# Second convolution by halves at its first and last channels, scan's first token piece loaded in parts, its first delta rows made by TensorE

## The chip, the cores and the metric

The kernel runs on one core of one Trainium2 chip. The core has five engines with instruction queues of their own: TensorE (PE in the profile, with PEld for its weight loads), VectorE (DVE), ScalarE (ACT), GpSimd (POOL) and SyncE (SP), which here only issues DMAs. Each queue is worked off in order: an instruction that waits for a semaphore holds all that stand behind it on its engine. The metric is the device time of one execution in microseconds (us), the median of three runs.

## What is computed

Two layers on a batch of 32 images of 96 channels, 56 by 56, all float32.

```python
# layer 0: depthwise 7x7, layer norm over channels, MLP 96 -> 384 -> 96, residual
h = conv_depthwise_7x7(x) + conv_b
h = layernorm_over_channels(h) * ln_g + ln_b
h = gelu(h @ w1 + b1) @ w2 + b2
x = layer_scale * h + x
# layer 1: depthwise 5x5, SiLU, selective scan over L = 3136 tokens
x = silu(conv_depthwise_5x5(x) + conv_b)
xs = x.reshape(B, C, L)
dts, Bs, Cs = split(einsum('kd,bdl->bkl', x_proj_w, xs))      # 6, 4, 4 rows
delta = softplus(einsum('dr,brl->bdl', dt_w, dts) + dt_b)
log_dA = maximum(delta * A, log(1e-9))                          # A: 96 x 4
P = exp(cumsum(log_dA))
hs = P * cumsum(delta * Bs * xs / maximum(P, 1e-9))
y = einsum('bdnl,bnl->bdl', hs, Cs) + xs * Ds
```

## The kernel before

The work has four stages one after the other: first convolution, MLP, second convolution, scan. Between stages the data pass through DRAM. A framework places buffers and semaphores; instructions that the code passes to `pin` keep the program's order on their engine, the others are placed by a scheduler.

**MLP (L487 to L589).** 28 groups of four image rows of half the batch. Half h = 0 is done first, then h = 1; within a half, `group(n)` (L152) gives row 0, 4, ... 24, each for two parts of the batch. Each group runs `hidden` (PE, then Gelu on ACT) and `result` (PE, then DVE adds bias and residual into a tile `o`). After the second part of a row group, POOL issues four DMAs for each of three channel blocks (L564), twelve in all, of 240 KB each, to `block_d`. Row m of `block_d` is (1 - h) * 28 + row + i: the first half fills rows 28 to 55, the second rows 0 to 27 upwards, so rows 24 to 27 come last. Rows stand in reverse: a high row of `block_d` is a low row of the image.

**Second convolution (L596 to L684).** 96 channels. `load_channel(c)` issues on SP the channel's taps (`wt`, L614, 128 KB) and two loads of 30 rows from `block_d` (`xq`, L626, 225 KB each): half h = 0 reads rows 26 to 55, half 1 rows 0 to 29. There are four pairs of `xq` buffers, zeroed once by DVE (L605), since the loads leave edges free. `convolve(c)` is 32 matmuls (L638), 16 for each half; `activate(c)` is one SiLU of 128 x 896 out of PSUM on ACT (L652); `beside` copies four residues of the columns into `st` (L661), one copy by ACT and three by DVE; `store_channel(c)` writes `conv2_d` (L667, 392 KB). `st` and `yt` have three buffers. The loop (L672) gives SP, for each c, the load of channel c + 2 and then the store of channel c - 2; both are on one queue, so the store stands behind that load and the next load behind the store.

**Scan (L692 on).** Tokens are taken in pieces of two images by 28 rows (`load(p)`, L723, tile `xs`); piece 0 goes by two DMAs on SP, one for each image. Each image of a piece makes three units of 128 rows: 32 channels by 4 states, 1568 tokens. For a unit:

- PE makes `pz` (L744) from the tokens, ACT turns it into delta by Softplus (L752), delta times token is made (L758; by DVE for the first image, by POOL after), and both are stored to `du_d` in DRAM (`keep_du`, L761)
- `spread_du` (L805) loads them back as `rep`, each channel's row four times, so that 128 rows stand side by side
- ACT's `decay` makes Exp, Relu, Identity of the delta rows (L810 to L812); POOL's `drive` multiplies the product rows by `bt` (L816); `bt` is spread by PE (L791) from rows that PE (L770) and a copy by ACT (L779) have made, and copied by ACT (L795)
- DVE runs two scans and one elementwise step (L826, L829, L833) through `pv` in PSUM, which is zeroed first (L699); POOL multiplies by `ct` (L845), PE sums (L855, L863), ACT copies and stores

The first image has its own sequence at L887 to L918. Its delta rows are stored and loaded back by themselves, ahead of the products: SP has the two delta stores, `spread_du(0, deltas)`, the two product stores, `spread_du(0, products)`, the rows of units 1 and 2 (both parts in one DMA each), then piece 1's tokens.

The loop and SP's order around the change:

```python
        for c in range(-2, C + 2):
            if c + 2 < C:
                load_channel(c + 2)
            if 0 <= c - 2:
                store_channel(c - 2)
            if 0 <= c < C:
                convolve(c)
...
                for h in range(2):
                    keep_du(0, h, deltas)
                spread_du(0, deltas)
                for h in range(2):
                    delta_x(0, h, nc.vector)
                    keep_du(0, h, products)
```

Of the kernel before, what the change touches and what calls it, by code (L numbers as in the profile page):

```python
# [21 lines left out]
N, R = 4, 6  # L22
# [27 lines left out]
def convnext_then_scan_kernel(  # L50
# [58 lines left out]
    dsm_t = const.tile([C, C], F32, name="dsm_t")  # L109

# [41 lines left out]
    def group(n):  # L152

        h, m = divmod(n, groups // 2)
        return h, m // 2 * RB, m % 2
# [20 lines left out]
    with tc.tile_pool(name="prep", bufs=1) as prep, tc.tile_pool(name="c1", bufs=4) as pool, tc.tile_pool(  # L176
# [145 lines left out]
        def scan_rows():  # L322
# [5 lines left out]
            for k in range(4):  # L328
                rows = slice(32 * k, 32 * k + 2 * N)
                at = 32 * k + (k // 2) * N  # L330
                kept(nc.vector.tensor_copy,
                    pick_t[rows].rearrange("p (d n) -> p d n", n=N),
                    ident[rows, at : at + N].rearrange("p (o n) -> p o n", o=1).to_broadcast(
                        [2 * N, DG, N]
                    ),
                )
            kept(nc.vector.tensor_reduce,
# [149 lines left out]
    with tc.tile_pool(name="mlp_g", bufs=14) as pool_g, tc.tile_pool(  # L487
# [46 lines left out]

        def result(n, s, d):
# [25 lines left out]
            if p == 1 and s == 1:  # L561
                m = (1 - h) * QR + row
                for i in range(RB):
                    nc.gpsimd.dma_start(  # L564
# [28 lines left out]

    with tc.tile_pool(name="c2", bufs=3) as pool, tc.tile_pool(  # L596
        name="c2k", bufs=1
    ) as keep, tc.tile_pool(name="c2_ps", bufs=4, space=PSUM) as psum:
# [4 lines left out]
        for t in xqs:  # L603
            for h in range(2):
                nc.vector.memset(t[h], 0.0)  # L605
# [4 lines left out]
        def load_channel(c):  # L610
            wt = pool.tile([128, RW * QC * 2], F32, name=f"wt2_{c}", tag="wt", bufs=4)
            taps = taps2_d[c, 0, 0:1, 0:1]
            step = QC * 2
            pin(nc.sync.dma_start(  # L614
                wt,
                bass.AP(
                    taps.tensor, taps.offset,
                    [[step, RW], [2 * RW * step, QC], [1, RW * step]],
                ),
            ))  # L620
            wts[c] = wt
            for h in range(2):
# [8 lines left out]
        def convolve(c):  # L631
            wv = wts.pop(c).rearrange("p (o f t) -> p f t o", f=QC, t=2)
            ps = psum.tile([128, 2, 512], F32, name=f"ps2_{c}", tag="ps")
            for h in range(2):
                xv = xqs[c % len(xqs)][h].rearrange("p (b r) -> p b r", r=QP)
                for t in range(2):
                    for f in range(QC):
                        pin(nc.tensor.matmul(  # L638
                            ps[RW * f : RW * f + RW, h, : B * QW].rearrange(
# [8 lines left out]
            pss[c] = ps  # L648

        def activate(c):  # L650
            yt = pool.tile([128, 2, B * QW], F32, name=f"yt_{c}", tag="yt")
            pin(nc.scalar.activation(  # L652
                yt, pss.pop(c)[:, :, : B * QW], AF.Silu, bias=c2b_t[:, c : c + 1], scale=1.0
            ))
            st = pool.tile([QR, 2, B, QW, QC], F32, name=f"st_{c}", tag="st")
            sts[c] = yt, st

        def beside(c, f, copy):

            yt, st = sts[c]  # L660
            pin(copy(  # L661
                st[:, :, :, :, f],
                yt[RW * f : RW * f + QR].rearrange("p h (b q) -> p h b q", q=QW),
            ))

        def store_channel(c):
            pin(nc.sync.dma_start(  # L667
                conv2_d[c].rearrange("(h o) w -> o h w", h=2),
                sts.pop(c)[1].rearrange("p h b q f -> p h (b q f)"),
            ))  # L670

        for c in range(-2, C + 2):  # L672
            if c + 2 < C:
                load_channel(c + 2)
            if 0 <= c - 2:
                store_channel(c - 2)
            if 0 <= c < C:
                convolve(c)
            if 0 <= c - 1 < C:
                beside(c - 1, 0, nc.scalar.copy)  # L680
            if 0 <= c < C:
                activate(c)
                for f in range(1, QC):
                    beside(c, f, nc.vector.tensor_copy)  # L684
# [7 lines left out]
    with tc.tile_pool(name="sc", bufs=2) as pool, tc.tile_pool(  # L692
# [10 lines left out]
        xts: dict = {}  # L703
# [9 lines left out]
        HQ = H // NCH  # L713
# [9 lines left out]
        def load(p):  # L723
            b, q = place(p * NI)
            xt = pool.tile([C, HQ, NI * W], F32, name=f"xs_{p}", tag="xs", bufs=3)
            rows = conv2_d[:, q * HQ : (q + 1) * HQ, b * W : (b + NI) * W]
            for i in range(1 if p else NI):
                cols = slice(None) if p else slice(i * W, (i + 1) * W)
                pin(nc.sync.dma_start(xt[:, :, cols], rows[:, :, cols]))
            xts[p] = xt  # L730

        def tokens(k, s, n):
# [3 lines left out]
            return xts[p][:, s * hh : (s + 1) * hh, i * W : (i + 1) * W]  # L736
# [40 lines left out]
        def rows_out(k):  # L777
            bn = pool.tile([128, 2, BK], F32, name=f"bn_{k}", tag="bn")
            pin(nc.scalar.copy(bn, bns[k][:, :, :BK]))  # L779
# [27 lines left out]
        def decay(i):  # L807

            g, da = i % NG, reps[i][:, 0, :]
            pin(nc.scalar.activation(da, da, AF.Exp, scale=a_t[:, g : g + 1]))  # L810
# [3 lines left out]
        def drive(i):  # L814
            ut = reps[i][:, 1, :]
            pin(nc.gpsimd.tensor_mul(ut, ut, bts[i // NG]))  # L816
# [66 lines left out]
        for i in range(-12, units + 1):  # L883
# [3 lines left out]
            if p == 0 and at == 0:  # L887
# [11 lines left out]
                spread_du(0, deltas)  # L899
                for h in range(2):  # L900
                    delta_x(0, h, nc.vector)
                    keep_du(0, h, products)
                rows_bc(0)
                rows_out(0)
                spread_du(0, products)
                for u in range(1, NG):
                    spread_du(u)
                load(1)
                for h in range(2):
                    spread(0, 0, h)  # L910
                decay(0)
# [7 lines left out]
            if at == 3 and p + 1 < PC and (p + 1) != 1:  # L919
                load(p + 1)  # L920
# [97 lines left out]
```

## Time and profile before

| what | value |
|---|---|
| median of three runs | 3308.79 us (3304.99 to 3313.47) |
| profiled execution | 3313.1 us, its span 3311.2 us |
| PE busy | 2783.1 us (84%) |
| DVE busy | 2593.7 us (78%) |
| ACT busy | 2240.1 us (68%) |
| POOL busy | 1685.9 us (51%) |
| first matmul of the second convolution | 1188.74 us from the span's start |
| its last matmul | ends at 1522.4 us |
| first scan of unit 0 (L826) | 1558.47 us |
| DMA in the middle of the second convolution (1300 to 1400) | busy share 0.93, 285 GB/s |

A line of a group of instructions reads: source line, engine, operation, what it writes <- what it reads with shapes, count | busy time in us, mean duration in ns | idle time of its engine just before, and what ended that idle time. A line of the order of time reads: start, length, engine, line, operation, tiles, count, and in brackets the idle time before it and what released it. SPq marks SP's issuing. The 40 digits are tenths of busy time in equal slices of the span, 82.8 us each.

### The profile page before, as it was taken

The numbers are of one execution on the slowest core, as the hardware profiler recorded it, in microseconds if no ns is written. First come the engines' busy times: TensorE is split into PE (matmuls) and PEld (weight loads), VectorE is DVE, ScalarE is ACT, GpSimd is POOL, SyncE is SP. The second block draws the span as 40 slices with busy tenths as digits, with TensorE's granted clock in tenths as the row PEclk, the third lists the DMA queues.
The fourth block names the chain that finished last, engine by engine and source line by source line (L and its number), as shares of the span: only waits on it lengthen the run. The fifth ranks groups of instructions, "written<-read, shape, count | busy, mean of one in ns | idle before, by whom it ended". The sixth has DMA issues, their size and how long they took to land. (4 is left out here: it accounts for less than half of the span.)

```text
span 3311.2 us, 53717 instructions
## 1 busy us (share of the span) xinstructions
PE 2783.1 (84%) x21898; PEld 1078.3 (33%) x21898; DVE 2593.7 (78%) x1538; ACT 2240.1 (68%) x1964; POOL 1685.9 (51%) x814
## 2 busy tenths in 40 slices
PE   8999899999999989994787777777777777777775
PEld 4666333333333333332222222222222222222221
DVE  7899533333333369996899999999999999999998
ACT  4556443333333358886888788888888887879784
POOL 1000010100101000001889899999989898989896
PEclk9999899999999999997666666666766666666767
DMA  8999765555646279998888777878787877778773
GB/s 246 292 295 292 208 177 153 168 164 148 183 138 188 76 213 288 286 283 227 285 279 266 270 257 272 283 254 279 253 282 254 286 253 274 256 272 268 271 269 110
DMA packets 299254, 788.03 MB, mean 238 GB/s; under 512 B 121648, under 2 KB 192176, under 8 KB 274464
## 3 DMA queue, kind: packets, MB, share of 16 engines
q1 hardware_dynamic: 263280, 659.77, 63.2%
q10 hardware_dynamic: 26896, 82.29, 6.7%
q0 software_dynamic: 8832, 42.55, 4.5%
q8 instruction: 172, 2.82, 0.4%
q14 instruction: 74, 0.61, 0.1%
HBM read 543.58 MB, written 240.90 MB: 237 GB/s over the span
## 5 line engine op out<-in xcount | busy, mean ns | idle before, releaser
L816 POOL TENSOR_TENSOR rep<-rep,bt 128x1568 f32<-128x1568 f32 x192 | 674.4, 3513 | 378.6 <-DMA rep<-du_d 378.6
L845 POOL TENSOR_TENSOR hs<-hs,ct 128x1568 f32<-128x1568 f32 x191 | 669.5, 3505 | 100.8 <-DVE hs L833 89.2
L826 DVE TENSOR_TENSOR_SCAN pv<-rep,pv 128x1568 f32<-128x1568 f32 x192 | 664.5, 3461 | 42.4 <-ACT rep L812 25.6
L530 ACT ACTIVATE g<-ph,b1p_t 128x896 f32<-128x896 f32 x336 | 320.2, 1004 | 483.8 <-PE ph L520 483.7
L553 DVE SCALAR_TENSOR_TENSOR o<-po,b2r_t,x 128x224 f32<-128x224 f32 x336 | 190.7, 608 | 530.1 <-PE po L539 523.2
L564 POOL DMA_DIRECT2D block_d<-o x168 | 81.1, 490 | 727.7 <-DVE o L553 622.0
L520 PE MATMUL ph<-h,w1r_t 32*128 32x448 f32 x4032 | 430.2, 555 | 4.4 <-ACT hs L403 2.3
L744 PE MATMUL pz<-xs,wd_t 96*96 96x392 f32 x512 | 280.9, 715 | 171.2 <-ACT du L752 120.1
L539 PE MATMUL po<-g,w_t 128*32 128x448 f32 x4032 | 413.1, 543 | 0.0
L791 PE MATMUL pk<-bn,pick_t 8*128 8x392 f32 x1024 | 291.9, 691 | 93.3 <-ACT y L872 81.4
L863 PE MATMUL py<-hs,sel_t 128*32 128x392 f32 x1536 | 322.7, 674 | 55.0 <-POOL hs L845 54.8
L829 DVE SCALAR_TENSOR_TENSOR pv<-pv,rep 128x1568 f32<-128x1568 f32 x192 | 345.6, 1800 | 21.3 <-POOL rep L816 1.4
L833 DVE TENSOR_TENSOR_SCAN hs<-rep,carry_h,pv 128x1568 f32<-128x1568 f32 x96 | 334.1, 3480 | 10.0
L661 DVE COPY st<-yt 28x896 f32<-28x896 f32 x288 | 317.9, 1104 | 26.9 <-ACT yt L652 13.1
L638 PE MATMUL ps<-xq,wt 128*32 128x448 f32 x3072 | 307.8, 546 | 37.1 <-DMA xq<-block_d 22.8
L833 DVE TENSOR_TENSOR_SCAN hs<-rep,pv 128x1568 f32<-128x1568 f32 x96 | 328.4, 3420 | 9.6
L375 PE MATMUL ps<-xt,mat 32*64 32x432 f32 (+2 forms) x6144 | 316.4, 556 | 22.6 <-ACT mat L357 22.2
L811 ACT ACTIVATE rep<-rep,lift_t 128x1568 f32<-128x1568 f32 x192 | 307.6, 1602 | 6.3
L812 ACT ACTIVATE rep<-rep,lift_t 128x1568 f32<-128x1568 f32 x192 | 307.6, 1602 | 6.3
L810 ACT ACTIVATE rep<-rep,a_t 128x1568 f32<-128x1568 f32 x192 | 308.3, 1606 | 4.7 <-DMA rep<-du_d 4.2
L855 PE MATMUL py<-xs,dsm_t 96*96 96x392 f32 x512 | 302.4, 732 | 10.0 <-ACT ct L795 4.5
L520 PEld LDWEIGHTS ph<-h,w1r_t 32*128 32x128 f32 x4032 | 192.7, 185 | 243.6 <-issue 155.8
(111 smaller groups left out, 2807.7 us busy)
## 6 DMA issues: line engine op xcount, KB each, us to landing
rep<-du_d SPq DMA_DIRECT2D x191, 1568.0 KB, 8.1
du_d<-du SPq DMA_DIRECT2D x126, 588.0 KB, 9.1
xq<-block_d SPq DMA_DIRECT2D x192, 225.0 KB, 5.1
xt<-in_x_dram SPq DMA_DIRECT2D x192, 224.0 KB, 4.9
block_d<-o POOLq DMA_DIRECT2D x168, 240.0 KB, 4.9
h<-conv_d SPq DMA_DIRECT2D x84, 448.0 KB, 5.1
x<-in_x_dram SPq DMA_DIRECT2D x336, 112.0 KB, 2.9
conv_d<-st SPq DMA_DIRECT2D x96, 392.0 KB
```

Source lines behind the costliest of these rows:

```text
L375: nc.tensor.matmul(pss[k // 2][2 * RW * p : 2 * RW * p + 2 * RW, k % 2, :HALF].rearrange("p (i r) -> p i r", r=W2)[:, :, lo:hi], lhsT=wv[r ...
L520: pin(nc.tensor.matmul(phs[i // 2][:, i % 2, :HALF], lhsT=w1r_t[rows, d, f * 128 : (f + 1) * 128], rhs=hts[n, d][rows, s * HALF : (s + 1) ...
L530: pin(nc.scalar.activation(gt, ph[:, :, :HALF], AF.Gelu, bias=b1p_t[:, f : f + 1], scale=1.0))
L539: pin(nc.tensor.matmul(po[CB * i : CB * i + CB, :HALF], lhsT=w2_t[:, f, CB * d : CB * d + CB], rhs=gts[n, s, f, i // 2][:, i % 2], start=( ...
L661: pin(copy(st[:, :, :, :, f], yt[RW * f : RW * f + QR].rearrange("p h (b q) -> p h b q", q=QW),))
L810: pin(nc.scalar.activation(da, da, AF.Exp, scale=a_t[:, g : g + 1]))
L816: pin(nc.gpsimd.tensor_mul(ut, ut, bts[i // NG]))
L826: pin(nc.vector.tensor_tensor_scan(grown, da, zero, pv[:, last : last + 1] if q else 1.0 / EPS, ALU.mult, ALU.add))
L829: pin(nc.vector.scalar_tensor_tensor(run, in0=grown, scalar=1.0, in1=ut, op0=ALU.min, op1=ALU.mult))
L833: pin(nc.vector.tensor_tensor_scan(ht, da, run, carry_h[:, col : col + 1] if q else 0.0, ALU.mult, ALU.add))
L845: pin(nc.gpsimd.tensor_mul(ht, ht, cts[k]))
L863: pin(nc.tensor.matmul(py[g * DG : (g + 1) * DG, s, :BK], lhsT=sel_t, rhs=hss[k * NG + g][:, cols], start=False, stop=True, tile_position= ...
```

## The change

Five edits, and helpers that go with them.

1. The MLP's second half takes its rows downwards, 24 to 0, so that rows 0 to 3 of `block_d` are written last; all but the last twelve stores on POOL are pinned.
2. The second convolution works by pieces: channels 0 to 3 by half 0, then channels 0 to 3 by half 1, then channels 4 to 94 whole, then channel 95 by half 0 and half 1: 101 pieces. SP is given load n + 3 and then store n - 2. Taps are loaded with a channel's first piece.
3. The `xq` buffers are zeroed by POOL, pinned, all halves 0 first; before it was DVE.
4. Piece 0's tokens: image 0 of channels 0 to 93 is loaded after channel 94's store has been issued, ahead of channel 95's stores; channels 94 and 95 after the last store; image 1 after the first image's product stores. The token pool is opened before the second convolution.
5. Unit 0's delta rows no longer pass through DRAM: four matmuls with a matrix of ones, `each_t`, repeat each of 32 channels four times in `pv`, and ACT's Exp reads them there in two instructions. The rows of units 1 and 2 are loaded in two DMAs each, deltas first. The copy of `bn` for image 0 goes from ACT to DVE.

```diff
-        return h, m // 2 * RB, m % 2
+        return h, ((QR - RB) - m // 2 * RB if h else m // 2 * RB), m % 2
...
+            kept(nc.vector.tensor_copy,
+                each_t.rearrange("p (d n) -> p d n", n=N),
+                ident[:DG, :DG].rearrange("p (d o) -> p d o", o=1).to_broadcast([DG, DG, N]),
+            )
...
+                store = early if n < groups - 1 else nc.gpsimd.dma_start
...
+    def load_tokens(p, channels=slice(0, C), images=slice(0, NI)):
+        b, q = p // NCH * NI, p % NCH
+        if p not in pieces_x:
+            pieces_x[p] = pool_xs.tile([C, HQ, NI * W], F32, name=f"xs_{p}", tag="xs")
+        cols = slice(images.start * W, images.stop * W)
+        rows = conv2_d[channels, q * HQ : (q + 1) * HQ, b * W : (b + NI) * W]
+        pin(nc.sync.dma_start(pieces_x[p][channels, :, cols], rows[:, :, cols]))
...
-        for t in xqs:
-            for h in range(2):
-                nc.vector.memset(t[h], 0.0)
+        for h in range(2):
+            for t in xqs:
+                pin(nc.gpsimd.memset(t[h], 0.0))
...
+        pieces = [(c, (h,)) for h in range(2) for c in range(len(xqs))]
+        pieces += [(c, (0, 1)) for c in range(len(xqs), C - 1)]
+        pieces += [(C - 1, (h,)) for h in range(2)]
...
-        for c in range(-2, C + 2):
-            if c + 2 < C:
-                load_channel(c + 2)
-            if 0 <= c - 2:
-                store_channel(c - 2)
+        for n in range(-3, last + 2):
+            if n + 3 < last:
+                load_piece(n + 3)
+            if 0 <= n - 2:
+                store_piece(n - 2)
+
+            if n - 2 == last - 3:
+                load_tokens(0, slice(0, C - 2), slice(0, 1))
...
+        load_tokens(0, slice(C - 2, C), slice(0, 1))
...
+        def delta_rows():
+
+            reps[0] = pool.tile([128, 2, CH], F32, name="rep_0", tag="rep", bufs=5)
+            at = pv.rearrange("p (s q) -> p s q", q=512)
+            for h in range(2):
+                for s in range(2):
+                    pin(nc.tensor.matmul(
+                        at[:, 2 * h + s, :BK], lhsT=each_t,
+                        rhs=dus[0, h][:DG, 0, s * BK : (s + 1) * BK],
+                        start=True, stop=True, tile_position=(0, 0),
+                    ))
+                pin(nc.scalar.activation(
+                    two(reps[0][:, 0, h * HT : (h + 1) * HT]), at[:, 2 * h : 2 * h + 2, :BK],
+                    AF.Exp, scale=a_t[:, 0:1],
+                ))
...
-                spread_du(0, deltas)
                 for h in range(2):
                     delta_x(0, h, nc.vector)
                     keep_du(0, h, products)
+                load_tokens(0, images=slice(1, 2))
+                delta_rows()
                 rows_bc(0)
-                rows_out(0)
+                rows_out(0, nc.vector.tensor_copy)
                 spread_du(0, products)
                 for u in range(1, NG):
-                    spread_du(u)
-                load(1)
+                    spread_du(u, deltas)
+                for u in range(1, NG):
+                    spread_du(u, products)
+                load_tokens(1)
+                decay(0, first=False)
                 for h in range(2):
                     spread(0, 0, h)
-                decay(0)
                 drive(0)
```

## The prediction

> **What bounds the kernel now.** I read the 40 slices first, then the idle times of the second convolution's groups, then the order of time at the stage's two ends.
>
> ```profile
> PE   8999899999999989994787777777777777777775
> ...
> DVE  7899533333333369996899999999999999999998
> ...
> DMA  8999765555646279998888777878787877778773
> ```
>
> Four stages: first convolution, MLP (DVE at 3), second convolution (slices 15 to 18: PE, DVE and DMA all at 9), scan (DVE at 9 to the end). Digits 13 to 14 and 18 to 19 are the seams. The scan is DVE's: 192 units of 3461 + 1800 + 3450 ns, with hardly a gap after 1634 us, so whatever moves the first units moves the end by as much.
>
> ```profile
> L661 DVE COPY st<-yt 28x896 f32<-28x896 f32 x288 | 317.9, 1104 | 26.9 <-ACT yt L652 13.1 <-DMA conv_d<-st 8.2 <-issue 0.2
> L638 PE MATMUL ps<-xq,wt 128*32 128x448 f32 x3068 | 307.1, 546 | 25.9 <-DMA xq<-block_d 22.8 <-ACT st L661 2.0
> L661 ACT COPY st<-yt 28x896 f32<-28x896 f32 x96 | 196.7, 2049 | 59.3 <-DMA conv_d<-st 58.1
> ```
>
> In the second convolution (window 1190 to 1530) DVE is busy 317.9 of 334 us; its only removable steady idle is the 8.2 us behind landing stores. PE's waits for loads and ACT's for stores lie beside that.
>
> ```profile
> 1174.58 1.93 POOL L564 DMA_DIRECT2D block_d<-o  x4 [44.11 <-DVE o L553]
> ...
> 1178.78 4.01 DVE L605 MEMSET xq<- 128x480 f32 x8
> 1179.03 1.45 POOL L564 DMA_DIRECT2D block_d<-o  x3 [0.26 <-DVE o L553]
> 1180.63 0.49 POOL L564 DMA_DIRECT2D block_d<-o  x1 [0.15 <-issue]
> 1180.66 2.14 SPq L626 DMA_DIRECT2D xq<-block_d  x2
> ...
> 1188.74 19.88 PE L638 MATMUL ps<-xq,wt 128*32 128x448 f32 x192 [11.19 <-DMA wt<-taps_d]
> ```
>
> The first seam: the last MLP rows are issued by POOL from 1174.58 to 1181.12, SP's first load of rows waits for them until 1180.66, and PE stands 11.19 us, until that load lands (7.7 us from issue, against 5.1 in the middle: twelve stores share the engines).
>
> ```profile
> 1521.86 2.90 DVE L661 COPY st<-yt 28x896 f32<-28x896 f32 x3 [0.42 <-DMA conv_d<-st]
> ...
> 1525.18 1.76 DVE L699 MEMSET pv<- 128x2048 f32 x1 [0.42 <-issue]
> 1526.96 2.85 DVE L661 COPY st<-yt 28x896 f32<-28x896 f32 x3
> 1533.41 2.39 SPq L729 DMA_DIRECT2D xs<-conv_d  x2
> ...
> 1539.67 4.71 PE L744 MATMUL pz<-xs,wd_t 96*96 96x392 f32 x8 [17.25 <-DMA xs<-conv_d]
> ...
> 1542.61 0.91 ACT L752 ACTIVATE du<-pz,dtb_t 96x784 f32<-96x784 f32 x1 [7.69 <-PE pz L744]
> ...
> 1553.57 1.60 ACT L810 ACTIVATE rep<-rep,a_t 128x1568 f32<-128x1568 f32 x1 [3.00 <-DMA rep<-du_d]
> ...
> 1558.47 3.43 DVE L826 TENSOR_TENSOR_SCAN pv<-rep,pv 128x1568 f32<-128x1568 f32 x1 [12.14 <-ACT rep L812]
> ...
> 1559.76 3.48 POOL L816 TENSOR_TENSOR rep<-rep,bt 128x1568 f32<-128x1568 f32 x1 [378.64 <-DMA rep<-du_d]
> ```
>
> The second seam is a serial chain: last copies, store, load of tokens (lands 5.6 later), PE at 1539.67, softplus, delta to DRAM and back as 128 rows, Exp at 1553.57, first scan 1558.47. Call PE's start P. After three units DVE idles again, 9.21 us before 1595.74: there ACT had first to serve the next token piece, issued at 1556.96 behind three row loads and landed at 1573.81 (P+34.1). A gain ahead of that is kept only if this piece comes earlier too.
>
> **Part A, the front: no early start, about -1.** The change lets half 0 of channels 0 to 3 read rows that were stored long before; but the loads wait for the zeroing, now on POOL, and in the built program the last twelve stores stand ahead of the eight memsets on POOL. So the first memset begins at 1181.1, not at 1168 when the hidden layer's inputs are free. POOL's memsets took 0.36 us for 288 columns and 1.69 for 1920, so 480 are some 0.5: first load near 1181.7, 1.0 late. Given back: the first SiLU needs 16 matmuls instead of 32 (4.74 us, at a granted clock of 0.5 to 0.8), some 1.9 sooner, and takes half of 1.0. Fifteen more DVE copies (thirty halves for fifteen whole ones) cost between nothing and 0.2 us each (the smallest instruction of ACT here, one column); I take 0.5 for them and POOL's delay together, since most lie beside other waits. Then halves 1 of channels 2 and 3 are issued only between stores that wait for DVE, while the queue has slack (DMA share 0.63 between 1195 and 1200). DVE, the fullest engine, so starts its first copy (1195.91) about 1.0 - 1.9 - 0.5 + 0.5 = -0.9 us from there, -1 rounded; from -2.5 (no lateness) to +2 (the slack is lost for good).
>
> The Trainium skill (Perfetto Trace Analysis, Optimizing Scalar/DVE Operations) speaks against halves: about 60 ns of access per DVE operation on SBUF. By it the copies would cost 15 x 0.06 = 0.9 us more (estimate); no row here has a half copy.
>
> **Part B, the middle: about -2.** Loads go out one piece further ahead (n+3 for c+2), now each behind the matmuls that free its buffer; the store stays behind them on SP's queue. This could end PE's 22.8 us of waiting, but DVE comes next, and has 8.2 us to give. DMA is at 0.93 to 0.94 there (1300 to 1500), and a row load takes SP 0.93 us to issue in the median where 0.32 is the fastest: near full. The cost side: SP waiting for PE delays the store queued behind it, and the three buffers of st are freed later. I bound it by doubling the same wait, +8.2; the other end is -8.2. I take -2: the nearest row, DVE at 95% of the window, says that little can change.
>
> **Part C, the last channel and the tokens: -4.5.** Old chain from the end of channel 94's copies: 1524.76, zeroing of pv, three copies, store 1529.87, landed about 1533.3, load, 1539.01, PE 1539.67. New: half 0 of channel 95 is copied first (3 x 0.55, half of 1.1) to 1526.4, and image 0 needs only that half; then pv and half 1, to 1529.9 as before. The 94-channel load goes out at about 1525.3, when channel 93's store (1521.50) has landed in some 3.5 us as the last one did; it takes 5.6, to 1531; half 0's store is behind it on the same queue, landed near 1531.8; then two channels, 2.6 us like the fastest small transfers (wt 2.5, du 2.6), 1534.5; PE at 1535.2. If the queue didn't matter, half 1's issue (1530.2) would set it: 1532.8, PE 1533.5, -6.2. If each of the two small transfers is held as the second image's load was (landed 2.88 after the one ahead, issued 0.37 after it), some 3.5 more: only -1 is left.
>
> The skill (DMA: Bandwidth & Descriptors, Queues, rings and completion order) says that an engine consumes one ring's descriptors in order: it backs the price of standing behind the big load, and by it -4.5 rather than -6.2 (estimate).
>
> **Part D, delta rows by TensorE: -4.9.** From P, by the rows above: the two softplus start at P+2.9 and P+4.75 (1542.61, 1544.42) and take 0.91; the table for Exp takes 1.28, to P+7.0; the four matmuls of 0.7 (nearest row: bt's, 0.71) lie beside that. Two Exp out of PSUM, 0.91 each as the softplus of the same 784 columns, to P+8.8; Relu and Identity, 1.6 each, to P+12.0: first scan there, before at P+18.8. But DVE's second step needs POOL's product, and its rows still come through DRAM. Before, the products' stores stood behind the delta row load on SP, so the product rows were issued at P+15.4 (1555.11). Now DVE has made both products at P+6.65, they are stored at P+6.7 and landed 2.9 later (a lone du store took 2.57): rows issued at P+9.6. Image 1's load stands ahead of them with 2.9 us of queue, so they land at P+15.1; POOL multiplies 3.5; second step at P+18.7 instead of P+23.6. The loads behind keep their old distances (landings 1559.7, 1563.93, 1568.52, 1573.81; split in two, but the same bytes): token piece 1 at P+29.2 instead of P+34.1, and unit 3, which waits for it, moves by the same 4.9.
> Beside it lie bt's copies (to P+13.7), bn's copy on an idle DVE, and image 1's softplus (to P+18.5, then table and decay to P+24.6; unit 1's scan would start at P+24.0, and unit 3's wait swallows the 0.6). Bounds: -2 (image 1's load pushes piece 1 back by all its 2.9) to -5.8 (not at all: P+15.4 to P+9.6).
>
> **Sum.** -1 - 2 - 4.5 - 4.9 = -12.4. The profiled execution took 3313.1 (span 3311.2 and 1.9 around it): 3300.7. The median of three runs is 4.3 lower, so I forecast 3296.
>
> **Rivals.**
> 1. The middle speeds up: PE's 22.8 us of load waits go and DVE's 8.2 with them: 6.2 more than forecast, 3290. For it: PE's idle names the loads; against: DVE and DMA near full. Chance 0.2.
> 2. The tail gives little: the big token load holds the last half's store and the two channels (C -1), and piece 1 doesn't come much earlier (D -2): -1 - 2 - 1 - 2 = -6, 3303. Several transfers in one queue speak for it, the lone landings of 2.5 us against. 0.23.
> 3. Slower: SP, now waiting for matmuls ahead of each load, issues the stores later, the three buffers of st come free later, and ACT (58.1 us of such waits already) and DVE lose that in each whole channel. A, C and D give 10.4, so it decides from 10.4 / 91 = 0.11 us for each of the 91; at 0.2 it is +18 - 10 = +8, 3317. Against: PE runs some 8 us ahead of the stores (channel 8: matmuls end 1218.8, store 1226.7), so its matmuls should be done when SP asks. 0.09.
> 4. The change does start the front early (memsets ahead of the stores): up to 8 more, 3288. The order on POOL speaks against. 0.03.
>
> **Numbers.** Forecast 0.45. A measurement can tell 0.3%, 9.9 us, from no change: faster means under 3298.9. The forecast lies just below, so two thirds of its 0.45 count as faster (0.30), with rivals 1 and 4 (0.23) and a little of rival 2: 0.56. Slower by as much is the larger part of rival 3, 0.05; the rest, 0.39, is no change. Range: all best ends are -2.5 - 8.2 - 6.2 - 5.8 = -22.7, 3286; at the other side 3309, no gain, beyond rival 2; most of rival 3 is left out.
>
> **What would show it.** A: memsets on POOL after 1181, PE's first matmul of the stage within 1 us of 1188.7. B: DVE idle in the middle near 8. C: PE's pz some 4.5 us nearer to the last matmul of the stage. D: first scan at P+12, second step P+18.7, the 9 us wait before unit 3 still there. Wrong if memsets run at 1168, if copies wait for stores more than before, or if piece 1 lands later than P+31.

## The result and the profile after

The changed kernel took 3326.7 us (median of four runs, 3323.6 to 3329.4), the kernel before 3311.1 beside it: 1.0046 times as long, 95% interval 1.0032 to 1.0061. The forecast was 3296, its range ended at 3309. With every execution of the kernel before that was run for this study (139, in six groups with medians from 3310.5 to 3312.4) its median is 3311.3, so the change costs 15.4 us. Executions of one kernel spread over 6 to 20 us; differences between two experiments therefore carry an interval, 95% by resampling the executions.

The profiled execution has a span of 3324.8 us, 13.6 more than before. In the 40 slices the stages look as before; at the second seam DVE's digit falls from 6 to 5 and DMA's from 8 to 6. Its timeline at the first seam, in the columns start, time, engine, line, tiles, count, [idle before and what ended it]:

```profile
1178.87 1.45 POOL L575 DMA_DIRECT2D block_d<-o  x3 [0.27 <-DVE o L562]
...
1181.02 3.59 POOL L632 MEMSET xq<- 128x480 f32 x8
1181.56 0.37 SPq L659 DMA_DIRECT2D xq<-block_d  x1
...
1188.88 10.42 PE L672 MATMUL ps<-xq,wt 128*32 128x448 f32 x84 [11.49 <-DMA xq<-block_d]
...
1194.15 4.91 DVE L698 COPY st<-yt 28x448 f32<-28x448 f32 x8 [15.58 <-ACT yt L687]
```

Up to here it is part A as forecast: zeroing behind the stores on POOL, PE 0.1 us later than before, DVE's first copy 1.8 us sooner. But the 1.8 us are lost again within the eight halves. DVE's timeline before (first line) and after:

```profile
1195.91 44.52 DVE L661 COPY st<-yt 28x896 f32<-28x896 f32 x39 [13.12 <-ACT yt L652]
...
1210.68 1.92 DVE L698 COPY st<-yt 28x448 f32<-28x448 f32 x3 [3.35 <-DMA conv_d<-st]
```

Before, 39 copies follow one another without a wait. After, the copies of the last half (channel 3) wait 3.35 us for a landing store; up to channel 10 such waits are 4.2 us in all, and twelve more copies keep DVE busy 1.9 us longer. So channel 10's first copy starts at 1234.6, before at 1230.1. The hidden layer's last matmul ends at 1168.2 and 1168.4 in the two profiles, so these 4.5 us arise in the second convolution. The copies as a group, busy 1.7 us longer than before:

```profile
L698 DVE COPY st<-yt 28x896 f32<-28x896 f32 (+1 forms) x303 | 319.6, 1055 | 32.2 <-ACT yt L687 15.6
```

The second seam, same timeline:

```profile
1527.60 0.23 SPq L615 DMA_DIRECT2D xs<-conv_d  x1
...
1528.68 17.67 SPq L706 DMA_DIRECT2D conv_d<-st  x2
1529.04 1.76 DVE L743 MEMSET pv<- 128x2048 f32 x1 [0.42 <-ACT st L698]
1530.82 1.67 DVE L698 COPY st<-yt 28x448 f32<-28x448 f32 x3
1548.34 0.24 SPq L615 DMA_DIRECT2D xs<-conv_d  x1
...
1550.46 5.30 PE L777 MATMUL pz<-xs,wd_t 96*96 96x392 f32 x8 [28.74 <-DMA xs<-conv_d]
```

The load of 94 channels is issued at 1527.60; the store behind it then holds SP from 1528.68, so that the last store goes out at 1546.01 though its copies ended at 1532.49. P, PE's start on the tokens, comes 10.8 us later than before, not 4.5 sooner. What the DMA engines did meanwhile, in a table by stretches (the last two columns are the share of 16 DMA engines and GB/s):

```profile
1530.00:1545.00 15.00, 0.00 (x0) 0.00 (x0) 2.45 (x4) 0.00 (x0) 0.00 (x0) 0.50 0.15 34
```

0.15 of 16 engines is about two, in a stretch in which almost only packets of 224 bytes ran. Before, the same kind of packet ran at a share of 1.18 (1534.40 to 1541.10; the share adds up the packets' times, so it can pass 1). After P:

```profile
1558.98 2.98 PE L846 MATMUL pv<-du,each_t 32*128 32x392 f32 x4 [1.72 <-ACT rep L851]
...
1566.21 3.43 DVE L876 TENSOR_TENSOR_SCAN pv<-rep,pv 128x1568 f32<-128x1568 f32 x1 [0.44 <-ACT rep L862]
...
1569.81 3.49 POOL L866 TENSOR_TENSOR rep<-rep,bt 128x1568 f32<-128x1568 f32 x1 [385.20 <-ACT bt L828]
```

The first scan is at P+15.8 (forecast P+12.0, before P+18.8), POOL's first product at P+19.4 waits for ACT's copies of the B rows and no longer for loaded rows, and unit 3 starts at P+55.3 (forecast P+51.2, before P+56.1): DVE still idles 7.43 us there, and ACT's Exp, Relu and Identity for this unit are what it waits for. Up to unit 16 DVE is 9.8 us behind the kernel before, at unit 191 it is 13.5 behind: 3.8 us are lost in the steady scan, where the change touches nothing.

### The profile page after: what moved, and what is told of

The parts are those of the page before. It is cut to its first block, busy times and chain, and to the rows that moved or that the text cites. A ratio compares the mean times of both kernels' runs of the same rounds, so it can differ in the third digit from the quotient of the medians.

```text
span 3324.8 us, 53793 instructions
## 1 busy us (share of the span) xinstructions
PE 2781.7 (84%) x21906; PEld 1081.9 (33%) x21906; DVE 2592.6 (78%) x1547; ACT 2239.2 (67%) x1974; POOL 1689.5 (51%) x822
## 5 line engine op out<-in xcount | busy, mean ns | idle before, releaser
L698 DVE COPY st<-yt 28x896 f32<-28x896 f32 (+1 forms) x303 | 319.6, 1055 | 32.2 <-ACT yt L687 15.6
L883 DVE TENSOR_TENSOR_SCAN hs<-rep,carry_h,pv 128x1568 f32<-128x1568 f32 x96 | 334.0, 3479 | 10.4 <-DVE pv L879 0.5
L672 PE MATMUL ps<-xq,wt 128*32 128x448 f32 x3072 | 305.9, 547 | 38.5 <-DMA xq<-block_d 30.6
```

What stands on the lines that cost most here:

```text
L698: pin(copy(st[:, :w, :, :, f], yt[RW * f : RW * f + QR, :w].rearrange("p h (b q) -> p h b q", q=QW),))
L883: pin(nc.vector.tensor_tensor_scan(ht, da, run, carry_h[:, col : col + 1] if q else 0.0, ALU.mult, ALU.add))
```

## The experiments

Theory: 94 and 2 channels get two DMA engines each, part D moves work onto ACT's and PE's chain, and the drift in the scan has a cause of its own. Rivals stand with each run. Every run is the changed kernel with the edit shown, unless it says otherwise.

### The split of the tokens

```diff
-                load_tokens(0, slice(0, C - 2), slice(0, 1))
+                load_tokens(0, slice(0, 80), slice(0, 1))
-        load_tokens(0, slice(C - 2, C), slice(0, 1))
+        load_tokens(0, slice(80, C), slice(0, 1))
```

> Only the split of image 0's first tokens changes: 80 channels early and 16 late, in place of 94 and 2. Theory 1 (94 and 2 channels are spread over two of the sixteen DMA engines, as the share of 0.15 over 17 us says, and SP is held by them): the first load takes about 5 us, SP isn't held by more than 1 us at the half store, PE's first pz matmul comes 14 to 15 us sooner relative to the last convolution matmul than in the changed kernel, and the time is about 3312 us. Theory 2 (a load of many 224-byte packets holds the store and the second load queued behind it, whatever the number of channels): 80 channels still hold SP some 80/94 of 17.2 = 14.7 us, and the time is about 3324 us.

3312.7 us, 14.0 less than the changed kernel (10.6 to 18.1): theory 1.

```profile
1529.54 0.37 SPq L615 DMA_DIRECT2D xs<-conv_d  x1
1530.88 4.20 SPq L706 DMA_DIRECT2D conv_d<-st  x2
1536.77 0.32 SPq L615 DMA_DIRECT2D xs<-conv_d  x1
```

80 channels landed 6.5 us after their issue, and P came 4.9 us behind DVE's last copy (18.0 in the changed kernel, 9.9 before).

Next, one load of 96 channels for image 0 behind the last store, and nothing early:

> Image 0's tokens are one load of 96 channels behind the last store; the second image's load and the delta rows stay as in the changed kernel. Both theories of the hold put PE's first pz matmul back to about 1539.7, 10.8 us sooner, and the time to about 3316 us. If the 10.8 us at the seam explain the whole loss apart from what the trace shows later in the scan (the shift grows by 3.7 us between unit 16 and unit 191), this is 3316 and not 3311; if that growth was a matter of one execution, it is about 3312.

3315.7 us: 11.0 less than the changed kernel (7.2 to 14.6), about the 10.8 us by which P had come late. The growth of the shift in the scan was there again (units 16 to 191: 1580.9 us; 1577.9 before, 1581.6 in the changed kernel), so it was not a matter of one execution.

The number of engines by itself: the kernel before, with fourteen loads behind its last store, each waiting for the one ahead.

```diff
+                for n in (96, 95, 94, 93, 92, 91, 90, 88, 86, 84, 80, 64, 16, 2):
+                    pin(nc.sync.dma_start(sizes[:n], conv2_d[:n, :HQ, :W]))
```

> The kernel before, and behind its last store fourteen loads of 28 rows of 56 from N channels of the second convolution's output into one spare tile, one after the other, with N = 96, 95, 94, 93, 92, 91, 90, 88, 86, 84, 80, 64, 16, 2 (the output isn't touched; its time isn't compared). Theory 1 (the channels are dealt to the largest number of engines up to 16 that divides N; 13 ns for each packet of 224 bytes of one engine, and 2.3 us fixed, estimated from the 17.2 us of 94 channels and the fastest small loads): 96: 4.5 us, 95 (5 engines): 9.2, 94 (2): 19.4, 93 (3): 13.6, 92 (4): 10.7, 91 (13): 4.8, 90 (15): 4.5, 88 (11): 5.2, 86 (2): 18, 84 (14): 4.5, 80: 4.1, 64: 3.8, 16: 2.7, 2 (2): 2.7. Theory 2 (nothing is special in 94; the seam's stores held it): durations fall smoothly from 4.5 to 2.7 us with N.

From issue to next issue: 96 channels 5.6 us, 95: 8.6, 94: 18.8, 93: 14.0, 92: 10.0, 91: 4.5, 90: 4.8, 88: 6.4, 86: 17.2, 84: 4.7, 80: 4.6, 64: 4.5, 16: 2.6. The shares of 16 engines, for 96, 95, 94, 93 and 90 channels in this order:

```profile
3304.70:3310.20 5.50, 0.00 (x0) 0.00 (x0) 0.00 (x0) 0.00 (x0) 0.00 (x0) 0.71 0.85 164
3310.30:3318.80 8.50, 0.00 (x0) 0.00 (x0) 0.00 (x0) 0.00 (x0) 0.00 (x0) 0.50 0.31 70
3318.90:3337.60 18.70, 0.00 (x0) 0.00 (x0) 0.00 (x0) 0.00 (x0) 0.00 (x0) 0.50 0.14 32
3337.70:3351.60 13.90, 0.00 (x0) 0.00 (x0) 0.00 (x0) 0.00 (x0) 0.00 (x0) 0.50 0.20 42
3366.30:3371.00 4.70, 0.00 (x0) 0.00 (x0) 0.00 (x0) 0.00 (x0) 0.00 (x0) 0.50 0.63 120
```

0.31, 0.14 and 0.20 are 5, 2 and 3 engines of 16: 95 = 5 x 19, 94 = 2 x 47, 93 = 3 x 31. Two channels fewer made the load more than three times as long, one fewer again made it shorter. The Trainium skill (DMA: Bandwidth & Descriptors, Why a DMA increments its semaphore by 16 and not by 1) states this rule, the largest number up to 16 that divides the outermost sizes of both sides. Times agree within 1.2 us of what the expectation made of it; for 88 channels (11 engines by the page) 6.4 us is nearer to 8 engines.

### What the convolution by halves is worth alone

Tokens and first image as in the kernel before; only pieces, prefetch and zeroing are changed.

> Only the second convolution is as in the changed kernel (pieces by halves, loads three pieces ahead, zeroing on POOL); tokens are loaded whole behind the last store, both images, and the first image's sequence is that of before. Theory 1 (parts A and B gave about 1 us, all of the loss is in the token split): 3309 to 3312 us. Rival (the convolution part is a loss of its own, which grows later as a shift of the scan): 3314 us or more.

3308.5 us, 2.8 less than all executions of the kernel before (5.0 to 0.2 less): on theory 1's side, a little below its range. Its own profile does not show where they come from: P stands 351.1 us after PE's first convolution matmul, before 350.9. Over all profiles of this study, two effects of the halves oppose each other. At the tail, P comes 11.6 to 12.0 us behind the end of channel 94's copies in the eight profiles with a halved last channel and whole token loads, 14.3 to 14.9 in the four with a whole last channel; its last store is half as large. At the front, channel 10's first copy comes 62.8 to 67.1 us behind the hidden layer's last matmul in the nine profiles with halves and POOL's stores, 60.7 to 61.8 in the three of the kernel before and its variants with POOL's stores. (Counted from that matmul, since its end lies between 1160.9 and 1169.4 from one execution to the next.)

### The rows through DRAM again

Part D undone in the changed kernel (`spread_du(0, deltas)`, first Exp from the loaded rows, `bn` copied by ACT).

> Unit 0's delta rows go through DRAM as before, the loads of rows take both parts at once again, ACT copies the B and C rows again; the split of the tokens (94 and 2) and the second image's late load stay. Theory 1 (part D gave only what the trace shows, 55.3 against 56.1 us from PE's first pz matmul to unit 3): 1 to 2 us slower than the changed kernel, about 3328 us. Rival (D gives its forecast 4.9 us but another part hides it): about 3331 us.

3322.4 us: 4.3 faster than the changed kernel (8.3 faster to 0.3 slower). Both theories expected it slower; part D was a loss, or this run had won something else. It had: units 16 to 191 took 1577.5 us again.

### The drift in the scan

In the changed kernel DVE stands still for 0.44 to 0.47 us in steady scan, 0.36 more than between its other steps, at DVE instructions 1471, 1599, 1727 ... 2495 of its stream, semaphore instructions counted: every 128th. One of them:

```profile
1761.05 3.49 DVE L876 TENSOR_TENSOR_SCAN pv<-rep,pv 128x1568 f32<-128x1568 f32 x1
1765.00 1.80 DVE L879 SCALAR_TENSOR_TENSOR pv<-pv,rep 128x1568 f32<-128x1568 f32 x1 [0.46 <-DVE pv L876]
```

The releaser named is the step itself, long done: nothing that the profile shows was waited for. Before, the 128th instruction is always a semaphore instruction, which waits beside a running scan, and no gap shows. Each unit gives DVE six instructions, three of them semaphores, and 128 is even: whether compute or semaphore is hit depends on whether the count ahead of the scan is odd, and part D's copy of `bn` on DVE had made it even.

```diff
                 warm = pool.tile([C, 1], F32, name="warm", bufs=1)
+                spare = pool.tile([C, 1], F32, name="spare", bufs=1)
+                pin(nc.vector.memset(spare, 0.0))
```

> The changed kernel with one more DVE instruction between the convolution and the scan (a memset of one column that nothing reads), put where DVE waits anyway. Theory (of the shift's growth in the scan): DVE pauses some 0.35 us at every 128th instruction of its stream; the change moved the stream by an odd number, so that the pause falls on a scan or multiply and no longer on a semaphore instruction that waits beside one. With one more, the nine pauses of 0.40 us at DVE instructions 1471, 1599, ... 2495 go, and the time falls by 9 x 0.35 = 3.2 us, to about 3323.5 us. Rival (the pauses come from data or from a neighbour engine, as the profile's releasers name them): they stay, and the time is 3326.7 us.

> The kernel before with the same one more DVE instruction at the same place. Theory: the nine or so pauses of 0.35 us now fall on scans and multiplies, and it is 3 us slower than before, about 3315.5 us, with gaps of 0.40 us every 128 DVE instructions. Rival: no gaps, 3312.4 us.

Neither told anything: the memset brought a semaphore instruction with it, two more in all. The gaps stayed in the one (3327.0 us), none came in the other (3314.1). With two memsets it is three instructions:

> The changed kernel with two more DVE memsets of one column between the convolution and the scan; they bring one semaphore instruction with them, so DVE's stream is three instructions longer ahead of the scan. Theory (every 128th DVE instruction costs a pause, hidden or not by whether the count ahead is odd): no gap of 0.40 us in the scan, unit 191 comes 1577.5 to 1578.5 us after unit 16 instead of 1581.6, and the time is 3323.5 us. Rival: gaps and time as in the changed kernel, 3326.7 us.

The nine gaps were gone, units 16 to 191 took 1578.7 us; the time, 3325.5 us, can't be told from 3326.7. A pair of the fastest kernel (below), with two memsets and with one:

> The run with the early front with one more one-column DVE memset between convolution and scan (two instead of one), so that the count ahead of the scan is even. Theory: nine pauses of 0.36 us in the scan, every 128 DVE instructions; 3.2 us slower than its pair, about 3306.5 us. Rival (the pauses are of the profiled execution only): the same as its pair within 1 us, about 3303.5.

> Its pair: the run with the early front again, one memset, odd count. Both theories: no pauses, about 3303.5 us.

The nine gaps are in the first, as here; in the second there is none at the same place:

```profile
1744.28 3.49 DVE L878 TENSOR_TENSOR_SCAN pv<-rep,pv 128x1568 f32<-128x1568 f32 x1 [0.44 <-ACT rep L862]
```

3307.3 and 3303.5 us: 3.9 more (0.8 less to 10.4 more). In all profiles the count decided without exception: even, nine gaps; odd, none. Units 16 to 191 take 1580.4 to 1582.8 us in the seven with an even count, 1577.1 to 1578.7 in the thirteen with an odd one. In the times the direction agrees with 9 x 0.36 = 3.2 us, the proof is not beyond doubt. The Trainium skill (Runtime: NRT & Kernel Launch, Instruction fetch mechanics) has instructions fetched in blocks of 256, "mostly hidden"; here the period is 128, and hiding depends on what the 128th is. That the pause is a fetch was not shown.

### Both images early

80 channels of both images in one load eight channels before the end, 16 behind the last store, the zeroing of `pv` behind the last copies; first with rows through DRAM, then by TensorE.

> Convolution by halves as in the changed kernel; both images' first 80 channels of tokens are one load eight channels earlier, the last 16 two loads behind the last store; the zeroing of pv on DVE stands behind the last copies instead of between the two halves of the last channel; the first image's sequence is that of before (rows through DRAM). Theory: with the 3308.5 us of the convolution alone, the zeroing off the path gives 1.8 us, the small last load 1.3 us more, the second image's rows ready as before: about 3305.5 us. Rival (a 1 MB load in the middle of the convolution delays row loads that are near full there, and DVE pays it): 3309 us or more.

> As the run with both images' 80 channels early, but with the changed kernel's first-image sequence (delta rows by TensorE), and one more DVE instruction for the pauses. Theory (what is bad in that sequence is the late load of the second image ahead of the product rows, and the pauses): first scan at P+15.7 as in the changed kernel, second step near P+20, and 1 to 3 us faster than the same kernel with rows through DRAM, about 3303.5 us. Rival (unit 1 and unit 3 are later with it whatever the load: units 1 to 3 wait for ACT, which has the same work and two more instructions): no faster or 1 us slower than that one.

3315.1 and 3316.0 us. Both are slower than the convolution alone, the first by 6.6 (3.1 to 10.9). P is 5.0 us behind the last copy, but that copy comes later (347.0 us after PE's first matmul against 344.7, 348.7 in the second): the rival's mechanism. From channel 10 to channel 94 DVE waits 13.2 and 15.1 us for landing stores, in the eighteen other profiles 3.8 to 10.9. And both have an even count, with its gaps.

### Why the halves did not start the front early

The twelve last stores move from POOL's queue to ACT's; convolution, tokens and first image as in the convolution alone.

```diff
-                store = early if n < groups - 1 else nc.gpsimd.dma_start
+                store = early if n < groups - 1 else at_once
+        def at_once(*args):
+            pin(nc.scalar.dma_start(*args))
```

> The convolution alone (as the run of that name), with the last twelve stores of the MLP issued by ACT, which idles there, instead of POOL; so POOL's zeroing waits no longer behind them, but only for the hidden layer's last matmul. Theory (the halves at the first channels give nothing because POOL's queue held their zeroing, and with it the first loads, until 1181): the zeroing starts near 1170, PE's first convolution matmul at 1176 to 1180 instead of 1188.9, DVE's first copy near 1183 to 1186 instead of 1194.2, and part of that is kept: 4 to 8 us faster than the 3308.5 us of the convolution alone, 3301 to 3304.5 us. Rival (DMA is the limit ahead: the second halves still wait for the last stores, and DVE then waits for loads): PE starts early, DVE idles later by as much, 3307 us or more. One more DVE instruction is added, with which the scan should show no pauses of 0.40 us.

```profile
1166.75 3.56 POOL L635 MEMSET xq<- 128x480 f32 x8 [38.04 <-PE ph L526]
...
1177.18 4.75 PE L675 MATMUL ps<-xq,wt 128*32 128x448 f32 x48 [1.39 <-issue]
...
1185.78 1.28 ACT L690 ACT_TABLE_LOAD   x1 [17.15 <-DMA block_d<-o]
...
1187.74 4.47 DVE L701 COPY st<-yt 28x448 f32<-28x448 f32 x7 [10.77 <-ACT yt L690]
```

3303.5 us, 0.9976 of the kernel before (0.9967 to 0.9985), 5.0 less than the convolution alone (8.3 to 1.6). Counted from the hidden layer's last matmul, PE starts 10.1 us sooner than in the changed kernel, DVE's copies 4.8: ACT's first SiLU now waits behind its own twelve DMA issues. Channel 10's first copy comes 57.7 to 61.5 us behind that matmul in the seven profiles with halves and ACT's stores, so that the front is back at the kernel before (60.7 to 61.8) or ahead of it. Run again as the pair's second kernel it took 3303.5 too. With the tokens split at 80 and 16 added:

> As the run with the early front, and the tokens' first 80 channels of both images in one load behind the store of channel 93, when no load of the convolution stands behind it any more, their last 16 in two loads behind the last store, and the zeroing of pv behind the last copies. DVE's count ahead of the scan is odd. Theory: PE's first pz matmul comes 4.9 us behind the last copy instead of 6.4, and the last copy 1.8 us sooner: 2 to 3 us faster than the run with the early front, about 3299 us, and faster than both kernels. Rival (a 1 MB load beside the last stores holds them, as 94 channels did): same as that run or slower.

3303.2 us: nothing more. P was 7.9 us behind the last copy instead of 6.3. The last 16 channels wait for the store of channel 95's first half and were issued 6.0 us behind it; where the 80 channels went eight channels earlier, it was 3.3. So the rival is nearer: a big load beside the last stores gives back what the split gains. The moved stores with whole channels, in the kernel before:

> The kernel before (whole channels) with the last twelve stores of the MLP issued by ACT and the zeroing on POOL. Theory (the early front needs both: queue free and halves that read rows stored long before): PE's first convolution matmul stays within 2 us of 1188.7, since a whole channel's rows include the last ones stored; no faster than 3311 us. Rival (it is only the queue and the sooner zeroing): 4 us or more faster, PE's first near 1183.

3307.8 us, 3.4 less than the kernel before (5.7 to 0.7), PE's first at 1182.1, DVE's first copy at 1194.0: nearly half of the 7.8 us between the kernel before and the early front seems to need no halves, though the interval is wide. The expectation, that nothing would come, was wrong. Where these 3.4 us come from is not shown: counted from the hidden layer's last matmul PE starts 4.7 to 5.2 us sooner than in the three profiles with POOL's stores, but DVE's first copy only 0.1 to 1.6 and channel 10 0.2 to 1.4.

### The delta rows by TensorE

On the kernel with the early front: part D with both images loaded behind the last store; the same with B and C rows ahead and all delta matmuls ahead of the Exps; part D absent, with only the second image's late load. All have the odd count.

> The run with the early front (3303.5 us, rows through DRAM) with the delta rows by TensorE put in, and both images' tokens loaded behind the last store, as there. Theory 1 (the second image's late load, which stands ahead of the product rows, ate part D's gain): first scan near P+15.5 instead of 18.7, unit 1 near P+26 instead of 29.3, unit 3 near P+52 instead of 55.8, and 3 to 4 us faster, about 3300 us. Theory 2 (ACT's and PE's queues: B and C rows and their copies stand behind the delta rows, so the product is late, and unit 3 waits for the next piece anyway): first scan P+15.5, unit 1 P+29 or later, unit 3 P+55 to 57, the time 3303 to 3305 us.

> As the run before, but the B and C rows go ahead of the delta rows on PE, their copies ahead of Relu and Identity on ACT, and all four delta matmuls ahead of the two Exps, so that no Exp stands between them. Theory 1: no further gain but for the 1.7 us wait between the halves, about 3299 us. Theory 2 (POOL's first product waited for ACT's copies of the B rows): first scan a little later (P+17), but POOL's first product 3 us sooner, unit 1 near P+26, and 1 to 3 us faster than the run before if unit 3 moves with it, else the same.

> The run with the early front (3303.5 us, rows through DRAM), with only the second image's tokens loaded late, behind the stores of unit 0's products. Theory 1: unit 0's product rows and unit 3 come 2 to 4 us later, 3306 us or more. Theory 2: no difference beyond 1 us, 3303.5 us.

3307.7, 3302.7 and 3304.5 us. Against the 23 executions without (3303.5): 4.3 more (0.9 to 6.9), 0.8 less (3.9 less to 3.4 more), 1.0 more (1.9 less to 5.0 more). So part D as written is a loss, in another order it is nothing, and the late load is small. ACT's timeline with part D, P = 1533.03:

```profile
1544.30 0.91 ACT L853 ACTIVATE rep<-pv,a_t 128x784 f32<-128x784 f32 x1 [3.07 <-PE pv L848]
...
1549.85 0.81 ACT L830 COPY bt<-pk 128x784 f32<-128x784 f32 x1 [1.37 <-PE pk L826]
...
1558.84 1.60 ACT L862 ACTIVATE rep<-rep,a_t 128x1568 f32<-128x1568 f32 x1
```

and without it, P = 1530.93:

```profile
1539.11 1.53 ACT L830 COPY bt<-pk 128x784 f32<-128x784 f32 x2 [1.03 <-PE pk L826]
...
1544.77 1.60 ACT L862 ACTIVATE rep<-rep,a_t 128x1568 f32<-128x1568 f32 x1 [2.82 <-DMA rep<-du_d]
...
1555.30 1.60 ACT L862 ACTIVATE rep<-rep,a_t 128x1568 f32<-128x1568 f32 x1 [1.34 <-DMA rep<-du_d]
```

Without it the copies of the B rows are done by P+9.7, inside the round trip through DRAM. With it they start at P+16.8, behind eight more matmuls on PE and two Exps; the softplus of the second image follows them, and unit 1's Exp starts at P+25.8 instead of P+24.4. Unit 0's scan is 3.3 us sooner, unit 1's 1.4 later (P+30.7 against P+29.3), unit 3's 1.9 later, unit 16's 3.5 later. One pair of executions may overstate this: unit 16 starts at P+174.6 to P+178.9 in the eight profiles with part D and at P+173.2 to P+176.9 in the twelve without, means 176.8 and 174.9. The changed kernel's own profile, with P+174.6, is the earliest of the eight. In the reordered run the second step waits for POOL no more, but the Exps wait 6.1 us for all matmuls, and the first scan itself comes at P+20.4.

## Why the prediction was wrong, step by step

| step | forecast | measured | from |
|---|---|---|---|
| A and B | -3 | -2.8 (-5.0 to -0.2), the smaller last store in it | convolution alone |
| C | -4.5 | +11.0 (+7.2 to +14.6) | whole load of image 0 behind the last store |
| D | -4.9 | +4.3 (+0.9 to +6.9) | part D on the early front |
| late load of image 1 | in D | +1.0 (-1.9 to +5.0) | late load alone |
| pauses of DVE | none | +3.2 (9 x 0.36, profile) | counts of DVE instructions |

The sum, 16.7, stands beside the measured 15.4, but that they are so close is luck: the intervals are wide, and in the changed kernel itself D and the pauses together gave 4.3 (the run with part D undone) where the table has 7.5. In the prediction's own terms, along the two profiles (one execution each), the shift is +2.1 at the end of channel 94's copies (A and B), +8.7 from there to P (C), -1.0 from P to unit 16 (D), +3.8 in the rest of the scan. The smaller last store, which the table has in its first row, belonged to the forecast of C.

- **A had the order right and the cost wrong.** The memsets stood behind POOL's stores, and PE's first matmul and DVE's first copy came as forecast. The step that failed is "I take 0.5 for them and POOL's delay together, since most lie beside other waits": after its first copy DVE had no such waits before, the additional copies took 1.9 us, and the 4.2 us in which halves waited for landing stores are not in the sum. Channel 10 came 4.5 us later, not 1 sooner. That the first row of the table meets its forecast is luck; what the profiles show as gained is at the tail. Copies that wait for stores more than before were among the forecast's own signs of being wrong. That the three buffers of `st`, now filled in half the time, are the reason is argued, not shown. The fourth rival named what the stores ahead of the memsets cost; moving them gave 5.0 of its "up to 8".
- **B** can't be told from nothing. From channel 10's first copy to the end of channel 94's it is 292.3 us, before 294.6; 292.9 to 298.8 in all four profiles with whole channels, 291.3 to 297.0 in the fourteen with halves and no 1 MB load in the middle. The third rival's losses in each whole channel are in no run. Nor are the first rival's gains: behind its first start, PE waited 19.1 us for loads, before 22.8.
- **C failed, and with it the sign.** The step is "it takes 5.6, to 1531": I took the duration of a load of 96 channels for one of 94. By the ladder it is 18.8, and in the changed kernel SP stood 17.2 us at the store behind it. The second rival saw the last store held by the load ahead, and priced it at 3.5 us, from a load on all engines. The skill page that I cited for the order in a queue has the engine count too; I did not divide. With 80 and 16 the part gives 3.0 us against the whole load (7.7 to 0.2; 3312.7 and 3315.7, both with the pauses).
- **D failed** in "Beside it lie bt's copies (to P+13.7)" and "lie beside that" for the matmuls. They do not: the second pair of matmuls waited 1.72 us for the first Exp, since both halves share the tile `pv`, then took 2.98 us where the first pair took 1.58, and the rows for B and C stood behind them. The second step came at P+22.9, not P+18.7. Unit 3 is set by ACT's queue, not by piece 1, which PE took up at P+30.6; so unit 3's wait swallowed the rest. That D gave nothing like its 4.9 us is shown; how much it lost is less sure: 4.3 by the pair on the early front, nothing in the other order, and in the changed kernel 4.3 together with the pauses.
- **The pauses** were in no step. The forecast of "bn's copy on an idle DVE" costed one instruction at nothing; it moved the count.
- The chances left 0.05 for slower by over 0.3%, all for a mechanism (stores behind loads in every channel) that did not occur.

## What to carry to other kernels

Before a load is split, factor its outermost size, here the number of channels: 94 ran on two engines (18.8 us), 80 took 4.6 us, and what is queued behind a load on two engines waits with it. An engine's earlier first instruction is no gain yet: follow the fullest engine to where its steady work begins. A step moved from a round trip through DRAM onto a compute engine is worth only what it brings the last thing that was hidden beside the round trip; list what now stands behind it on each engine. When queue order stops an edit, move the other instruction: the convolution by halves was worth 3 us, with the stores on an idle engine's queue 8, and that kernel (3303.5 us) beats both.

## What the runs showed of the hardware

- In the scan, DVE stands 0.36 us longer at every 128th instruction (1471 to 2495) where that is a scan or an elementwise step, and shows no gap where it is a semaphore instruction; one instruction more can so cost 3.2 us (9 x 0.36) far from its place.
- PE's granted clock after the idle stretch ahead of P is not the same in each execution. In the first 4.6 us from P it is 0.50 to 0.61. In the next 3.4 us it was 1.00 in the kernel before and in the early front, but 0.50 in the latter's twin with the even count, and in seven others. Without part D, unit 3 came at P+56.8 to P+57.7 where it was 0.50, at P+55.5 to P+56.6 in seven profiles where it was 0.90 or more, but at P+57.6 in an eighth, the ladder's, with 1.00. With part D it was 0.50 to 0.55 from P+8 to P+20 in all eight profiles, though PE was busy throughout in the reordered run; part of what part D loses may lie there. What decides the clock stays open, as does its share in the spread between executions.
- A load on two engines holds the issue of the next DMA on its queue: in the four profiles with 94 channels loaded ahead of a store, SP stood 17.2 to 17.3 us at that store.
